# One core: global attention, then a perception layer with local attention; a half of the local values moves between two guide jobs, taps go by a table, bounds are watched by sums of VectorE's own results

## The chip, the cores and the metric

The kernel runs on one core of a Trainium2 chip, in float32. The metric is the device time of one execution in microseconds. A core has TensorE (PE, the matmuls; its weight loads are shown apart as PEld), VectorE (DVE), ScalarE (ACT), GpSimd (POOL) and SyncE (SP, which here only issues DMAs). Each engine works through its own queue in order, and waits on semaphores for the others.

## The reference

Layer 0 is self-attention over the 4096 pixels of each of four images of 64 x 64 x 256. Layer 1 is a depthwise 3x3 convolution with three outputs per channel, an MLP (768 to 512 to 256, gelu) with a residual, and a 3x3 local attention with a residual.

```python
q = x @ Wq + bq; k = x @ Wk + bk; v = x @ Wv + bv
attn = softmax(einsum('bnd,bmd->bnm', q, k), axis=-1)
out = gamma * einsum('bnm,bmc->bnc', attn, v) + inputs          # layer 0

perceived = conv3x3_depthwise(x, w_perc) + b_perc               # 256 -> 768
hid = gelu(einsum('bphw,dp->bdhw', perceived, w_up1) + b_up1)   # 768 -> 512
h = x + einsum('bdhw,cd->bchw', hid, w_up2) + b_up2             # 512 -> 256
q, k, v = split(einsum('bhwc,dc->bhwd', h, w_qkv) + b_qkv, 3)
scores = stack([(q * shifted(k, dy, dx)).sum(-1) for dy, dx in POS]) / 16
out = h + sum(softmax(scores)[i] * shifted(v, *POS[i]))         # layer 1
```

## The kernel before

Pixels lie in 32 blocks of 512 (8 rows of an image), channels on the partitions. The time goes into `unshifted()`, which computes both softmaxes without subtracting a maximum. So that this is safe, it watches its own values: `watch` adds them on GpSimd into a tile `watched`, and at the end a sum of that tile decides whether a second, slower program (`shifted()`, not run here) is needed.

The loop over `slot` handles one block of global attention per slot, in 16 points. At each point TensorE gets, in this order: at even points four `energy` matmuls (`e`, L294), then the jobs of the point, then eight matmul passes of `product` (`acc`, L313). ScalarE takes the exponential of a half of `e` (`p`, L302), VectorE adds `p` into the denominator `den` (L327, one per point). Blocks that are further on run beside it as jobs: with `k = slot - 3`, `hidden_part` (first MLP matmul), `update_part` (second, giving `h`), `guide_part` (query and key weights joined: `lq = wg h`), `scores`, `local_values`, `border`; with `a = slot - 5`, `local_product` and the output. Several of these 2x2 block products are done with seven instead of eight multiplications: `update_part` and `guide_part` have the parts ab, cd, eg, f, and mixes of the inputs are formed on VectorE before (`guide_mix` writes the four `gmix`) and results gathered after (`gather`, L537 and L539).

The convolution (`perceive`) is a generator. Tap 0 of an output runs on ScalarE (L464), each further tap is one scalar_tensor_tensor on VectorE (L468), and four mixes per third (L474) follow: 60 steps per slot. After each point's jobs, product and `den` add, the loop takes steps until `stepped` reaches `to`. So VectorE's queue in a point is: the adds of the point's jobs, the `den` add, the point's taps.

All PSUM banks of jobs come from `job_bank`, and in the loop that is one tag `m` with two buffers, taken in turn: a job's matmul waits until the bank used two jobs ago has been read.

At the end of a slot, `partial_sums` and `finish` turn the denominator into its inverse (`dps`, a matmul of 32 columns), scale `acc` into `o` (L378) and add it to the image in `xp` (L383). `border_terms` and `border` compute the scores that padded neighbours would have: VectorE forms `edge` (L855, L856, four instructions, eight where the block touches the image's upper or lower edge), TensorE sums it over partitions with a matmul by ones (`c`, L867). After the loop, the last blocks go through the same functions with less around them (`run(...)`): there `local_values` of the last block also watches squares of `lv`, and `local_total` sums the local weights on TensorE (`ld`, L994). The three uses of `watch` that the change touches stand in `finish`, `scores` and `local_product`.

Of the kernel before, what the change touches and what calls it, by code (L numbers as in the profile page):

```python
# [15 lines left out]
P = 128  # L16
# [16 lines left out]
MULT = 3  # L33
# [19 lines left out]
def attention_then_perception_kernel(  # L53
# [26 lines left out]
        return t  # L80

    ones = const.tile([P, P], F32, tag="ones", name="ones")
    watched = const.tile([P, C], F32, tag="watched", name="watched")
    bad = const.tile([P, 1], mybir.dt.int32, tag="bad", name="bad")


# [1 line left out]
    def unshifted():  # L88
# [92 lines left out]
        def watch(values):  # L181

            n = values.free_size()
            for i in range(0, n, C):
                at = watched[:, : min(C, n - i)]
                nc.gpsimd.tensor_tensor(at, at, values[:, i : min(n, i + C)], ALU.add)  # L186


        queries, keys, values, staged = {}, {}, {}, {}
# [170 lines left out]
        def finish(s, parts=((0, RB),)):  # L360

            acc = accs.pop(s)
            n = NJ * (1 if shared(s) is None else 2)
            ps = bank("m", f"dps_{s}")[:, :n]
            given = parts_.pop(s).rearrange("p i j -> p (i j)")[:, :n]
            nc.tensor.matmul(ps, lhsT=fold, rhs=given, start=True, stop=True)
            inverse = tile_of([P, 2, NJ], "inverse", f"inverse_{s}")
            inverses[s] = inverse
            nc.vector.reciprocal(inverse.rearrange("p i j -> p (i j)")[:, :n], ps)

            rden = sums.pop(s)[:, 1, :]
            on_all(inverse[:, 0, :], turneds[s][:, 0, :], rden)
            watch(inverse.rearrange("p i j -> p (i j)")[:, :n])
            os = [tile_of([P, NB], "o", f"o_{s}_{c}", 2) for c in range(CH)]
            for r0, r1 in parts:
                n = slice(r0 * W, r1 * W)
                for c, o in enumerate(os):
                    nc.vector.scalar_tensor_tensor(  # L378
                        o[:, n], acc[c][:, n], gam[:, 0:1], rden[:, n], ALU.mult, ALU.mult
                    )  # L380
                for c, o in enumerate(os):
                    dst = xv[:, c, ring(s) + r0 : ring(s) + r1, 1 : 1 + W]
                    nc.vector.scalar_tensor_tensor(  # L383
                        dst, o[:, n].rearrange("p (h w) -> p h w", w=W), gbv[:, c : c + 1], dst,
                        ALU.add, ALU.add,
                    )
                if len(parts) > 1:
                    yield
            if s < NSLOT - 1:
                rim(s)  # L390
            for o in os:
                watch(o)
            yield

        def rim(s):
# [226 lines left out]
        def pixels(s, c):  # L622
            return hs[s][:, c, :, HALO:, :].rearrange("p a h w -> p h a w")
# [39 lines left out]
        def update_part(s, part):  # L663


            if part == "ab":
                below(s)
            b11, b12, b21, b22, mix1 = update_mixes[s]
            y11, y12, y21, y22 = (lambda j, y=y: y[:, j] for y in blocks_of(wup2, CH, P))
            t1, t2, t4 = (lambda j, i=i: wmix2[:, i, j] for i in range(3))  # L670
            v11, v12, v21, v22, v1 = (lambda j, b=b: b[:, j] for b in (b11, b12, b21, b22, mix1))
            todo = dict(
                ab=((y11, v11), (y21, v21)), cd=((t2, v11), (y12, v12)),
                eg=((t1, v1), (t4, v22)), f=((y22, v21),),
            )[part]
            ps = seven(f"dx_{s}_{part}", CH, *todo)
            if part == "ab":
                nc.vector.tensor_tensor(b11, mix1, b11, ALU.subtract)
                nc.vector.tensor_tensor(b21, b21, b11, ALU.subtract)
            gather(  # L680
                part, [by_rows(t) for t in ps],
                *(quarter(s, c, n) for n in range(2) for c in range(2)), None,
            )
            if part == "f":
                for c in range(CH):
                    for half in range(2):
                        h = hs[s][:, c, half, HALO:, :]
                        at = 1 + half * KW
                        nc.vector.scalar_tensor_tensor(
                            h, h, bup2[:, c : c + 1],  # L690
                            xv[:, c, ring(s) : ring(s) + RB, at : at + KW], ALU.add, ALU.add,
                        )
                guide_mix(s)
                border_terms(s)

# [162 lines left out]
        def border(s):  # L860


            ps = job_bank(f"c_{s}")
            row = edge_row(s)
            n_side = 2 * RB
            n = border_parts(s)[-1][0].stop
            nc.tensor.matmul(ps[:, :n], lhsT=ones, rhs=edge[:, :n], start=True, stop=True)  # L867
            one = pad[0:1, :]
            nc.scalar.activation(one[:, :n], ps[0:1, :n], AF.Exp, bias=bc, scale=-(C**-0.5))
            nc.gpsimd.tensor_scalar(one[:, :n], one[:, :n], 3.0, None, ALU.mult)  # L870
            if row is not None:

                ends = one[:, n_side : n : W - 1]
                nc.gpsimd.tensor_scalar(ends, ends, 2.0 / 3.0, None, ALU.mult)
# [39 lines left out]
        def scores(s, half):  # L914
# [19 lines left out]
            else:  # L934
# [7 lines left out]
                    p = late[s][:, half * C : half * C + QR * QW]  # L942
            near_ws[s, half] = p.rearrange("p (t h w) -> p t h w", h=QR, w=QW)
            nc.scalar.activation(p[:, :n], ps[:, :n], AF.Exp, scale=C**-0.5)  # L944
            engine = nc.vector if s >= NSLOT - 2 else nc.gpsimd
            pv = p[:, :n].rearrange("p (t n) -> p t n", t=tiles)
            mask = near[:, half, :rows, :].rearrange("p h w -> p (h w)")
            engine.tensor_tensor(  # L948
                pv, pv, mask.unsqueeze(1).to_broadcast([P, tiles, rows * QW]), ALU.mult
            )  # L950

            if g == 0:
                nc.gpsimd.memset(p[P // 2 :, : UP * QW], 0.0)
                if s < NSLOT:
                    nc.gpsimd.memset(p[: P // 2, UP * QW : QR * QW], 0.0)
            if s >= DIRECT:

                watch(p[:, :n])

# [48 lines left out]
        def local_product(s, c, behind=None):  # L1008
            b, g = divmod(s, NBLK)
            ps = job_bank(f"lo_{s}_{c}")  # L1010
            pv = ps.rearrange("p (h w) -> p h w", w=W)
            todo = [(half, *piece) for half in range(2) for piece in pieces(s)]
            for i, (half, (block, t), rows, of) in enumerate(todo):
                nc.tensor.matmul(  # L1014
                    pv[:, rows, columns(half)],
                    lhsT=lvs[block, t, half][:, bass.ts(c, P)],
                    rhs=near_ws[block, half][:, t, of, :],
                    start=(i == 0), stop=(i == len(todo) - 1), skip_group_check=True,
                )
            if behind:  # L1020
                behind()
            if s < DIRECT:
                o = tile_of([P, NB], "o", f"lo_{s}_{c}", 2)
            else:
                o = tile_of([P, 2, NB], "p", f"lo_{s}_{c}", 3)[:, 0, :]
            nc.vector.tensor_tensor(o, ps, lrdens[s], ALU.mult)  # L1026
            if s < NSLOT - 1:
                watch(o)
            engine, res = nc.gpsimd, o
            if s >= DIRECT:  # L1030

                if c == 0:
                    results[s] = tile_of([P, CH, NB], "xc", f"res_{s}", 2)
                engine, res = nc.vector, results[s][:, c, :]
            ov, rv = (t.rearrange("p (h a w) -> p h a w", a=2, w=KW) for t in (o, res))
            engine.tensor_tensor(rv, ov, pixels(s, c), ALU.add)
            nc.sync.dma_start(out=out[b, :, c, bass.ts(g, NB)], in_=res)

        def job(f, s, *args, n=NSLOT):
            return [lambda: f(s, *args)] if 0 <= s < n else []  # L1040
# [33 lines left out]
        for slot in range(NSLOT):  # L1074
            b, g = divmod(slot, NBLK)
            if slot >= RING:
# [6 lines left out]
                job(hidden_part, k, 1, 0), job(hidden_part, k, 1, 1),  # L1083
                job(local_product, a, 0), job(local_product, a, 1) + job(update_mix, k),
                job(update_part, k, "ab"), job(update_part, k, "cd") + job(update_part, k, "eg"),
                job(update_part, k, "f"), job(guide_part, k, "ab") + job(guide_part, k, "cd"),
                job(guide_part, k, "eg") + job(guide_part, k, "f"), job(scores, k, 0),
                job(scores, k, 1) + job(local_sum, k - 1), job(local_values, k, 0), job(border, k), [],
            ]
            if slot in (1, 2):  # L1090
                jobs[0] = [lambda: next(combine)] * 2
# [7 lines left out]
            conv = perceive(slot - LAG_PERC, mixed) if slot >= LAG_PERC else iter(())  # L1099
            n_mixed = NPC * (TAPS - 1) + MULT * len(MIXED)  # L1100
            n_steps, stepped = n_mixed, 0
            if slot == NSLOT - 1:

                nc.sync.dma_start(out=wup2[:, :CH, P:], in_=w_up2[:, :CH, P:])
# [20 lines left out]
            for point in range(points):  # L1125
# [17 lines left out]
                else:  # L1143
                    partial_sums(slot)

                to = min(n_steps, -(-(point + 1) * n_steps // (points - 2)))
                if point < 3:

                    to = min(to, n_mixed // MULT)
                while stepped < to:  # L1150
                    next(conv, None)
                    stepped += 1
# [492 lines left out]
```

## Time and profile before

| | us |
|---|---|
| Median of three runs | 3489.54 (3489.46 to 3489.93) |
| The profiled execution's own time | 3489.6 |
| Its span, first to last instruction | 3487.6 |
| TensorE busy | 3454.0 |
| VectorE busy | 2796.8 |
| ScalarE busy | 1063.4 |
| GpSimd busy | 694.3 |

The mean granted TensorE clock is 0.999. A slot without projections for the next image lies 103.1 us after the one before by its `dps` matmul, eight of them 104.0; slots 7, 15 and 23, which also project the next image, take 137. In the profile a row of groups gives the line, engine, operation, what is written from what, the number of instructions, the busy time and the mean of one; a float32 matmul shows as two passes, so counts are doubled. In a timeline, the columns are start, length, engine and line, and in brackets the idle time before and what ended it. Matmul ends are modelled and overlap the next start, so the distance from start to start is the better measure of what TensorE takes.

Groups that the change touches:

```profile
L186 POOL TENSOR_TENSOR watched<-watched,lo 128x256 f32<-128x256 f32 x124 | 136.8, 1103 | 1015.8 <-DVE lo L1026 1010.7
L186 POOL TENSOR_TENSOR watched<-watched,o 128x256 f32<-128x256 f32 x128 | 109.6, 856 | 43.2 <-DVE o L378 35.7
L1036 POOL TENSOR_TENSOR lo<-lo,h 128x512 f32<-128x512 f32 x56 | 96.2, 1719 | 4.4
L1026 DVE TENSOR_TENSOR lo<-lo,lrden 128x512 f32<-128x512 f32 x64 | 43.8, 685 | 66.5 <-PE lo L1014 66.2
L378 DVE SCALAR_TENSOR_TENSOR o<-acc,gam,den 128x512 f32<-128x512 f32 x62 | 43.7, 747 | 1.6 <-DVE den L358 0.5
L867 PE MATMUL c<-edge,ones 128*128 128x16 f32 x48 | 9.3, 270 | 0.0
```

### The profile page before, as it was taken

What the parts mean: (1) busy time and instruction counts of PE and PEld (TensorE: products, weight loads), DVE (VectorE), ACT (ScalarE), POOL (GpSimd) and SP (SyncE); (2) the same over time, 40 slices, a digit from 0 to 9 for tenths busy, and PEclk for the clock granted to TensorE, in tenths of its full rate; (3) what the DMA queues carried; (4) which work ended last, traced back from release to release, by engine and by line L of the source; (5) the groups of instructions that cost most, each with busy time, mean ns of one, the idle gap of its engine ahead of it and who ended that gap; (6) DMA issues with size and microseconds to landing.
All of it is one profiled execution on the core that took longest, in us unless ns stands there. A gap on an engine that the chain in (4) does not pass through costs nothing. (4 is left out here: it accounts for less than half of the span.)

```text
span 3487.6 us, 34030 instructions
## 1 busy us (share of the span) xinstructions
PE 3454.0 (99%) x12726; PEld 1995.1 (57%) x12726; DVE 2796.8 (80%) x4249; ACT 1063.4 (30%) x1328; POOL 694.3 (20%) x829
## 2 busy tenths in 40 slices
PE   9999999999999999999999999999999999999998
PEld 5445555555555555566555555556655555555655
DVE  2388888768888988876888889887688888888886
ACT  3233333323332233332333322333233333223331
POOL 2010112111221221121112212212121121221133
PEclk9999999999999999999999999999999999999999
DMA  4000000120000000011000000001100000000000
GB/s 106 7 4 10 7 9 16 32 47 20 9 16 7 16 16 16 22 25 46 16 9 16 10 13 16 16 22 31 39 16 16 16 10 7 16 16 17 7 7 25
DMA packets 93276, 67.06 MB, mean 19 GB/s; under 512 B 65872, under 2 KB 71248, under 8 KB 92976
## 3 DMA queue, kind: packets, MB, share of 16 engines
q1 hardware_dynamic: 92432, 64.42, 6.8%
q8 instruction: 102, 1.67, 0.2%
q14 instruction: 70, 0.57, 0.1%
q10 hardware_dynamic: 672, 0.39, 0.0%
HBM read 43.62 MB, written 18.81 MB: 18 GB/s over the span
## 5 line engine op out<-in xcount | busy, mean ns | idle before, releaser
L313 PE MATMUL acc<-p,v 128*128 128x512 f32 x4096 | 1838.6, 594 | 0.2 <-DVE o L378 0.2
L313 PEld LDWEIGHTS acc<-p,v 128*128 128x128 f32 x4096 | 768.2, 190 | 795.8 <-issue 779.6
L468 DVE SCALAR_TENSOR_TENSOR perc<-xp,wperc,perc 128x512 f32<-128x512 f32 (+2 forms) x1554 | 1166.7, 811 | 7.0 <-ACT perc L464 7.0
L302 ACT ACTIVATE p<-e 128x1024 f32<-128x1024 f32 x512 | 523.9, 1023 | 1695.0 <-PE e L294 776.9
L327 DVE TENSOR_TENSOR den<-den,p 128x1024 f32<-128x1024 f32 x480 | 604.6, 1259 | 85.4 <-ACT p L302 83.6
L186 POOL TENSOR_TENSOR watched<-watched,lo 128x256 f32<-128x256 f32 x124 | 136.8, 1103 | 1015.8 <-DVE lo L1026 1010.7
L948 POOL TENSOR_TENSOR lp<-lp,near 128x396 f32<-128x396 f32 x60 | 77.5, 1291 | 1137.9 <-ACT lp L944 1132.9
L294 PE MATMUL e<-qa,ka 32*128 32x512 f32 x2048 | 291.9, 640 | 0.0
L474 DVE TENSOR_TENSOR perc<-perc 128x256 f32<-128x256 f32 x360 | 174.3, 498 | 7.2
L294 PEld LDWEIGHTS e<-qa,ka 32*128 32x128 f32 x2048 | 80.0, 182 | 166.2 <-issue 164.2
L573 PE MATMUL hid_de<-perc,wmix 128*128 128x256 f32 x720 | 165.2, 379 | 0.0
L573 PEld LDWEIGHTS hid_de<-perc,wmix 128*128 128x128 f32 x720 | 136.8, 190 | 43.7 <-issue 21.5
L580 DVE TENSOR_TENSOR hid<-hid_bc,hid 128x512 f32<-128x512 f32 x60 | 41.5, 692 | 147.4 <-PE hid_bc L573 147.3
L596 ACT ACTIVATE hid<-hid,bup 128x512 f32<-128x512 f32 x120 | 80.1, 715 | 214.3 <-DVE hid L580 214.3
L464 ACT ACTIVATE perc<-xp,bperc,wperc 128x512 f32<-128x512 f32 x192 | 145.4, 807 | 0.0
L969 POOL TENSOR_TENSOR lsum<-lsum,lp 128x99 f32<-128x99 f32 x168 | 132.0, 792 | 11.0
L1014 PEld LDWEIGHTS lo<-lp,lv 128*128 128x128 f32 x732 | 102.9, 191 | 35.1 <-issue 27.0
L883 PE MATMUL lv<-wlv,h 128*128 128x256 f32 x520 | 122.4, 379 | 0.0
L186 POOL TENSOR_TENSOR watched<-watched,o 128x256 f32<-128x256 f32 x128 | 109.6, 856 | 43.2 <-DVE o L378 35.7
L302 ACT ACT_TABLE_LOAD x60 | 77.0, 1283 | 134.1 <-PE e L294 134.1
L260 PE MATMUL v<-wv,xc 128*128 128x256 f32 x512 | 116.3, 380 | 0.1
L883 PEld LDWEIGHTS lv<-wlv,h 128*128 128x128 f32 x520 | 98.7, 190 | 27.5 <-issue 15.5
(191 smaller groups left out, 3398.8 us busy)
## 6 DMA issues: line engine op xcount, KB each, us to landing
xp<-in_x SPq DMA_DIRECT2D x30, 528.0 KB, 4.1
xc<-in_x SPq DMA_DIRECT2D x56, 256.0 KB, 3.7
out<-lo SPq DMA_DIRECT2D x56, 256.0 KB, 2.1
qa<-packed SPq DMA_DIRECT2D x124, 64.0 KB, 2.0
out<-res SPq DMA_DIRECT2D x8, 256.0 KB, 2.0
ka<-st SPq DMA_DIRECT2D x124, 16.0 KB, 1.8
packed<-st SPq DMA_DIRECT2D x31, 64.0 KB, 1.9
wup<-in_w_up SPq DMA_DIRECT2D x1, 1536.0 KB, 6.8
```

The costliest lines, as they stand in the source:

```text
L186: nc.gpsimd.tensor_tensor(at, at, values[:, i : min(n, i + C)], ALU.add)
L260: nc.tensor.matmul(ps[:, i * C : (i + 1) * C], lhsT=xc[:, kin, bass.ts(2 * pair + i, P)], rhs=wv[:, kin, :], start=(kin == 0), stop=(kin = ...
L294: nc.tensor.matmul(e[:, j, :], lhsT=key[rows, :], rhs=queries[s][rows, :], start=True, stop=True,)
L302: nc.scalar.activation(p, energies[s, G][:, 2 * half : 2 * half + 2, :], AF.Exp)
L313: nc.tensor.matmul(accs[s][c], lhsT=v[:, 2 * half + i, bass.ts(c, P)], rhs=p[:, i, :], start=(first and i == 0), stop=(G == NG - 1 and hal ...
L327: nc.vector.tensor_tensor(den, den, p, ALU.add)
L464: nc.scalar.activation(acc, win, AF.Identity, bias=bperc[:, half, j : j + 1], scale=wt)
L468: nc.vector.scalar_tensor_tensor(acc, win, wt, acc, ALU.mult, ALU.add)
L474: nc.vector.tensor_tensor(t[:, to, :], t[:, a, :], t[:, b, :], op)
L573: nc.tensor.matmul(ps[:, n * C : (n + 1) * C], lhsT=w(j), rhs=mixes[s, j][:, kind, :], start=(j == 0), stop=(j == MULT - 1),)
L883: nc.tensor.matmul(ps[:, half * C : (half + 1) * C], lhsT=keys_of(s, t, half, kin), rhs=wlv[:, kin, :], start=(kin == 0), stop=(kin == CH ...
L969: nc.gpsimd.tensor_tensor(to, to, near_ws[block, half][:, t_, of, :], ALU.add)
```

## The change

It has five parts.

- `job(local_values, k, 0)` moves from point 13 to point 9, between the parts ab and cd of `guide_part`. `border_terms` leaves `update_part` (point 8) and becomes the job of point 13.
- In all slots but the last, the steps of the convolution follow a table `share` of steps per point instead of an even division.
- `finish`, `local_product` and, in the last two blocks, `scores` no longer watch on GpSimd. The VectorE instruction that writes the value also writes the sum of what it wrote into a column of `watched` of its own (`accum_out`); tensor_tensor becomes scalar_tensor_tensor for that. What GpSimd still watches, it adds in pieces of 128 columns instead of 256.
- The residual of the local attention runs on VectorE in all blocks, where GpSimd had it in most.
- The matmul `c` of `border` has one column of ones as weights and writes one partition.

```diff
+    WATCHED = P + 4 * NSLOT + 6
+    watched = const.tile([P, WATCHED], F32, tag="watched", name="watched")
...
-            for i in range(0, n, C):
-                at = watched[:, : min(C, n - i)]
-                nc.gpsimd.tensor_tensor(at, at, values[:, i : min(n, i + C)], ALU.add)
+            for i in range(0, n, P):
+                at = watched[:, : min(P, n - i)]
+                nc.gpsimd.tensor_tensor(at, at, values[:, i : min(n, i + P)], ALU.add)
+        free = iter(range(P, WATCHED))
+        def seen():
+            i = next(free)
+            return watched[:, i : i + 1]
...
-                        o[:, n], acc[c][:, n], gam[:, 0:1], rden[:, n], ALU.mult, ALU.mult
+                        o[:, n], acc[c][:, n], gam[:, 0:1], rden[:, n], ALU.mult, ALU.mult,
+                        accum_out=seen(),
...
-            for o in os:
-                watch(o)
...
                 guide_mix(s)
-                border_terms(s)
...
-            nc.tensor.matmul(ps[:, :n], lhsT=ones, rhs=edge[:, :n], start=True, stop=True)
+            nc.tensor.matmul(ps[0:1, :n], lhsT=ones[:, 0:1], rhs=edge[:, :n], start=True, stop=True)
...
-            engine = nc.vector if s >= NSLOT - 2 else nc.gpsimd
+            if s < NSLOT - 2:
+                nc.gpsimd.tensor_tensor(pv, pv, mask, ALU.mult)
+            else:
+                nc.vector.scalar_tensor_tensor(
+                    pv, pv, 1.0, mask, ALU.mult, ALU.mult, accum_out=seen()
+                )
...
-            if s >= DIRECT:
+            if DIRECT <= s < NSLOT - 2:
                 watch(p[:, :n])
...
-            nc.vector.tensor_tensor(o, ps, lrdens[s], ALU.mult)
             if s < NSLOT - 1:
-                watch(o)
-            engine, res = nc.gpsimd, o
+                nc.vector.scalar_tensor_tensor(
+                    o, ps, 1.0, lrdens[s], ALU.mult, ALU.mult, accum_out=seen()
+                )
+            else:
+                nc.vector.tensor_tensor(o, ps, lrdens[s], ALU.mult)
+            res = o
...
-            engine.tensor_tensor(rv, ov, pixels(s, c), ALU.add)
+            nc.vector.tensor_tensor(rv, ov, pixels(s, c), ALU.add)
...
-                job(update_part, k, "f"), job(guide_part, k, "ab") + job(guide_part, k, "cd"),
+                job(update_part, k, "f"),
+                job(guide_part, k, "ab") + job(local_values, k, 0) + job(guide_part, k, "cd"),
                 job(guide_part, k, "eg") + job(guide_part, k, "f"), job(scores, k, 0),
-                job(scores, k, 1) + job(local_sum, k - 1), job(local_values, k, 0), job(border, k), [],
+                job(scores, k, 1) + job(local_sum, k - 1), job(border_terms, k), job(border, k), [],
...
+            share = [6, 7, 7, 5, 4, 3, 3, 3, 2, 2, 4, 5, 5, 4, 0, 0]
...
-                to = min(n_steps, -(-(point + 1) * n_steps // (points - 2)))
-                if point < 3:
-                    to = min(to, n_mixed // MULT)
+                if slot < NSLOT - 1:
+                    to = sum(share[: point + 1])
+                else:
+                    to = min(n_steps, -(-(point + 1) * n_steps // (points - 2)))
+                    if point < 3:
+                        to = min(to, n_mixed // MULT)
```

## The prediction made before the result was known

> **What bounds the kernel now.** I read the page's busy table first, then the waits by engine, then the timelines of TensorE (PE) and VectorE (DVE) through one stretch of 103 us between two `dps` matmuls (one slot), then the timelines of the last 70 us.
>
> ```profile
> PE 3454.0 (99%) x12726; PEld 1995.1 (57%) x12726; DVE 2796.8 (80%) x4249; ACT 1063.4 (30%) x1328; POOL 694.3 (20%) x829
> ```
>
> TensorE is idle for 3487.6 - 3454.0 = 33.6 us of the span. A change that leaves its matmuls alone can win only there. The waits view says where:
>
> ```profile
> PE g_cd L525 <- DVE gmix L798: 13.4, 23, 0.7
> PE s L924 <- DVE lq L539: 5.0, 8, 0.7
> PE ld L994 <- POOL lp L953: 1.8, 1, 1.8
> PE ld L994 <- DVE lp L948: 1.5, 1, 1.5
> PE ld L994 <- DVE lv L948: 1.0, 1, 1.0
> ```
>
> The columns are total, times, longest. The first two recur by slot, the last three stand in the last 75 us. The first is larger than it looks, since a matmul's end is modelled. From the TensorE timeline (slot 20; columns start, length):
>
> ```profile
> 2123.65 1.13 PE L525 MATMUL dx_f<-hid,wup 128*128 128x256 f32 x4
> 2124.61 3.60 PE L313 MATMUL acc<-p,v 128*128 128x512 f32 x8
> 2128.05 1.16 PE L525 MATMUL g_ab<-h,wg 128*128 128x256 f32 x4
> 2129.79 1.10 PE L525 MATMUL g_cd<-gmix,gmix 128*128 128x256 f32 x4 [0.58 <-DVE gmix L798]
> ```
>
> g_ab starts at 2128.05 and g_cd 1.74 later; in the five of 28 slots without the wait it is 0.86. So the stall is 0.88 to 0.90 each, and over all 28 slots these distances exceed 0.86 by 20.7 us in sum. In the same way the eight `acc` before the first `s` take 4.3 instead of 3.43 us in eight slots, 3.51 in most others: 7.4 us in sum. VectorE in the same slot:
>
> ```profile
> 2126.45 0.42 DVE L537 TENSOR_TENSOR h<-dx_f,h 128x256 f32<-128x256 f32 x1
> 2126.79 1.67 DVE L689 SCALAR_TENSOR_TENSOR h<-h,bup,xp 128x256 f32<-128x256 f32 x4
> 2128.55 0.76 DVE L798 TENSOR_TENSOR gmix<-h 128x256 f32<-128x256 f32 x2
> 2129.22 0.42 DVE L798 TENSOR_TENSOR gmix<-gmix,h 128x256 f32<-128x256 f32 x1
> ...
> 2130.83 1.22 DVE L327 TENSOR_TENSOR den<-den,p 128x1024 f32<-128x1024 f32 x1
> ...
> 2133.88 0.48 DVE L539 SCALAR_TENSOR_TENSOR lq<-g_ab,small,lq 128x256 f32<-128x256 f32 x1
> ```
>
> VectorE takes dx_f up at 2126.45 without idling, while TensorE left it at 2124.61: it is 1.64 us behind (in slot 7, 15 and 23, where it idles, it starts 0.20 after). The third gmix ends at 2129.64 and g_cd starts 0.15 later.
>
> **What the Trainium skill says.** "VectorE: DVE Perf Modes", section "Two Vector instructions with no wait between them": an instruction that also writes out its accumulator is two, the main one and an accumulator read. No run here shows it; the nearest tiny VectorE operation, the edge term of 8 elements, takes 0.23 us, 0.15 start to start. "Vector Engine (DVE) Microarchitecture Reference", section "Points that are easy to get wrong", says scalar_tensor_tensor with two non-bf16 SBUF sources halves throughput. The trace doesn't bear this out without a sum: such taps take 0.665 us apart for 512 elements, as tensor_tensor does. "SBUF — State Buffer", section "SBUF: two separate sides", says VectorE with two SBUF inputs and GpSimd lock each other out of a shared port. That agrees: beside GpSimd's watching, four taps at 2106.82 took 3.75 us, 0.94 each.
>
> **Part 1, the table of taps and the work taken to VectorE.** Prices, start to start: tap 0.665, den 1.13, mix step 0.41, 512-wide operation 0.61 (0.72 if it waits for the one before), accumulator read 0.15 to 0.25 (I take 0.2; ends 0 and 0.6, the last if the sum halves the rate). Points 0 to 4 get 29 steps for 22, points 5 to 9 get 13 for 21, points 10 to 13 get 18 for 17. The seven early ones (4.7 us) fall where VectorE idles 0.88 + 0.97 + 0.46 + 4.18 + 1.48 + 1.44 = 9.4 us in this slot. The first hid_de add comes about 0.7 later (2076.6 to 2077.3); its PSUM bank is next wanted at 2081.87. Both versions meet at the hid_gf add at 2094.67, which waits for TensorE. From there, by hand: 2095.3; den 2096.4; ScalarE's first tap of the next tile, behind two gelus, 2097.6; five taps 2100.9; local product 0 with sum and residual (0.61 + 0.2 + 0.72) 2102.5; den 2103.6; four taps 2106.3; product 1 2107.8; two update mixes 2109.2; den 2110.3; three taps 2112.3; dx_ab is ready at 2112.4, three adds 2114.1; den and three taps 2117.2; dx_cd ready 2117.5, then dx_eg ready 2119.25 with three adds 2120.5; den, tap and two mixes 2123.1. dx_f is ready at 2124.8. VectorE therefore waits there 1.7 us where it was 1.64 us late. The residual (56 times 0.7 = 39 us) and the sums (four a slot, 128 x 0.2 = 26 us) are on no path as long as that margin stands. GpSimd loses 136.8 + 109.6 + 96.2 = 343 us, on no path outside the end. The output DMA on SP waits for VectorE at 2102.5 and 2107.8 instead of GpSimd at 2105.7 and 2112.0: earlier, so nothing behind it on that queue is late.
>
> **Part 2, the first half of local values between ab and cd.** It moves four matmuls (eight passes, 1.73 us by L883) and two VectorE adds (0.74) from point 13 into point 9; no DMA. TensorE's count is unchanged. g_cd is now wanted 3.44 + 0.86 + 1.73 = 6.03 us after dx_f's end. gmix is ready by 0.20 + 3.2: far covered. But job banks are two in turn: with the values between, g_cd gets g_ab's bank, so it must wait until VectorE has read g_ab (lq L539). Before it in VectorE's queue: 0.20 latency, dx_f add to last gmix 3.57 (2126.45 to 2130.02), den 1.13, two mixes 0.78, itself 0.48, and 0.15 to TensorE: 6.31. ScalarE's copy of g_ab, which it also needs, ends at 2130.12, that is 5.51: not later. Stall 6.31 - 6.03 = 0.28; I take 0.3 (0 to 0.9). It strikes all 28 slots, the five clean ones too: 8.4, with 0.08 restart in five, 9 us. The wait is shared by everything queued on TensorE. Gain 20.7 - 9 = 11.7 us.
>
> **Part 3, border terms to point 13.** Four or eight operations of 0.23 us leave the way to lq. The lq chain after g_f (three adds, 1.85) ends at 2139.5, and s_0 is due at 2141.3. So the 7.4 us go, the edge slots included. At point 13 the border's matmul follows one point later, over 3 us. The slot's end idles 2.15 us on VectorE; +0.66 for a tap, +0.8 for borders (1.6 in edge slots), -0.74 for the values: hidden.
>
> **Part 4, border sum into one partition.** The two c passes take 0.25 us to the next acc. Weight loads of one column took 81 ns in L753 against 190. I take 0.1 x 32 = 3 us (0 to 4).
>
> **Part 5, the end.** GpSimd is the chain from 3460.65 to 3474.76. The watch of the last block's two `lp` (four rows from 3470.30 to 3473.36, 3.1 us) leaves it; each of six squares is now watched in two pieces of about 0.46 (the row of 140 columns takes 0.56, that of 99 takes 0.40) instead of one of 0.73, + 0.25 with the gap, 1.5 in all; the ld stall of 1.81 falls to about 0.2. The stalls at 3415.6 and 3418.2 give back some 0.4, since GpSimd's watching no longer slows the taps between, less 0.2 for sums. TensorE's clock reads 0.56 and 0.59 in 3419 to 3423: about 1.7 us lost, which I leave standing (gain 0 to 1.7). Together 2 us (0.5 to 4).
>
> **Sum.** 11.7 + 7.4 + 3 + 2 = 24 us from the profiled execution's 3489.6 (span 3487.6 and 2.0 around it), which equals the median shown, 3489.54: 3466.
>
> **Rivals.** (a) The bank wait keeps nearly all of the old stall, because sums cost more or a wait in the queue before lq is longer than read: 28 x 0.7 = 19.6 instead of 9, 3477. For: the chain has thirteen instructions; against: each was measured. (b) No bank wait, lq being early: 9 back, 3457. Against: two banks in turn. (c) Slower: VectorE stays behind at dx_f as now. Every 1 us of delay is 28 us. The gains without the stall are 20.7 + 7.4 + 3 + 2 = 33; at (0.28 + L) x 28 = 33, thus L = 0.9, it is even. At today's L = 1.64 the stall is 1.92, 54 us, which gives 3511. It takes 1.7 + 0.9 = 2.6 us more than I counted between points 3 and 7, where the two sums and two residuals stand; even the sums at half rate bring 0.8. (d) The early taps stall hid banks: they would have to come 4 us later, not 0.7.
>
> **Numbers.** Main case 0.70, 3466 (own range 3460 to 3471); (a) 0.14; (b) 0.08; (c) and (d) 0.05, the rest small gains under 7 us. Range 3456 to 3477. No change means within 0.2%, 7 us, what a measurement can tell here. Faster 0.92, same 0.03, slower 0.05.
>
> **What would show it.** Right: g_cd no longer waits for gmix; a wait of about 0.3 us on lq in all 28 slots, slots of 103.1 and 104.0 us becoming about 102.4 both; VectorE idle before dx_f; no s wait; ld's wait on GpSimd under 0.5. Wrong: VectorE without idle at dx_f, accumulator rows above 0.6 us, or waits of acc or hid on VectorE in points 0 to 3.

## The result and the profile after

The changed kernel takes 3457.85 us (median of four runs, 3457.53 to 3457.90), the kernel before 3489.73 beside it: a ratio of 0.9908, 95% interval 0.9891 to 0.9925. That is 31.9 us less, where the prediction had 24 us and 3466. The profiled execution has a span of 3455.9 us at a granted clock of 0.999, so the spans differ by 31.7 us. The page after, busy times (share of the span) and instruction counts:

```profile
PE 3442.0 (100%) x12726; PEld 1995.0 (58%) x12726; DVE 2736.2 (79%) x4439; ACT 1063.8 (31%) x1328; POOL 355.7 (10%) x525
```

TensorE runs the same 12726 matmul passes and idles 3455.9 - 3442.0 = 13.9 us instead of 33.6; its busy time fell too, by 12 us, so the idle time alone doesn't count the gain. In part that is because a group that runs up to a stall is recorded longer (g_ab in slot 20 had 1.16 us before and has 1.03 now); `c` and `hid` became shorter as well. GpSimd lost half of its work. The waits after (total, times, longest):

```profile
...
PE ld L1005 <- DVE lp L959: 0.8, 1, 0.8
PE g_cd L534 <- DVE lq L548: 0.5, 2, 0.4
...
PE ld L1005 <- POOL lp L964: 0.4, 1, 0.4
```

The two repeated waits of before, of g_cd for gmix and of s for lq, are gone. There is a new releaser of g_cd, the addition to lq at L548. The view counts it twice; the distances from lv to g_cd show it in every slot (1.87 to 2.26 us, where lv alone takes 1.73). TensorE in slot 20 (start, length):

```profile
2107.52 3.60 PE L323 MATMUL acc<-p,v 128*128 128x512 f32 x8
2110.95 1.03 PE L534 MATMUL g_ab<-h,wg 128*128 128x256 f32 x4
2111.82 1.89 PE L891 MATMUL lv<-wlv,h 128*128 128x256 f32 x8
2113.70 1.13 PE L534 MATMUL g_cd<-gmix,gmix 128*128 128x256 f32 x4
2114.67 3.60 PE L323 MATMUL acc<-p,v 128*128 128x512 f32 x8
```

From lv to g_cd it is 1.88 us, where eight passes of lv take 1.73. VectorE in the same slot:

```profile
2107.72 0.42 DVE L546 TENSOR_TENSOR h<-dx_f,h 128x256 f32<-128x256 f32 x1 [1.51 <-PE dx_f L534]
...
2110.89 0.42 DVE L806 TENSOR_TENSOR gmix<-h,gmix 128x256 f32<-128x256 f32 x1
2111.24 1.22 DVE L337 TENSOR_TENSOR den<-den,p 128x1024 f32<-128x1024 f32 x1
2112.37 0.88 DVE L483 TENSOR_TENSOR perc<-perc 128x256 f32<-128x256 f32 x2
2113.17 0.48 DVE L548 SCALAR_TENSOR_TENSOR lq<-g_ab,small,lq 128x256 f32<-128x256 f32 x1
```

VectorE now idles 1.51 us and takes dx_f up 0.20 after TensorE left it (1.84 before). The last gmix is done at 2111.31, over two us before g_cd wants it. The addition to lq ends at 2113.65, and g_cd starts 0.05 later: this is the wait for the bank.

Start-to-start distances on TensorE, summed over the 31 slots between the first and the last `dps`, say where the loop's 28.0 us come from. "Predicted" is the term of the prediction's sum.

| Sites in the loop | before, us | after, us | gain | predicted |
|---|---|---|---|---|
| g_ab, with the wait of g_cd for gmix behind it | 44.8 | 24.2 | 20.6 | 20.7 |
| lv, with the wait of g_cd for the bank | 103.6 | 108.5 | -4.9 | -8.4 |
| g_cd's own extent | 25.9 | 27.1 | -1.2 | -0.4 |
| acc before s, with the wait of s for lq | 107.0 | 99.6 | 7.5 | 7.4 |
| s and g_f, their own extents | 97.4 | 93.0 | 4.4 | 0 |
| c | 7.3 | 4.5 | 2.8 | 3 |
| other acc | 1626.9 | 1627.8 | -0.9 | 0 |

Outside the loop, the stretch from the last `dps` to the end went from 120.2 to 117.0 us, and the start gave 0.5, with a DMA that landed earlier. A slot without projections takes 102.1 us (103.1 before), one at the image's edge 102.2 (104.0), one with projections 137.2 (137.0).

### The profile page after: what moved, and what is told of

The parts are those of the page before. It is cut to its first block, busy times and chain, and to the rows that moved or that the text cites. A ratio compares the mean times of both kernels' runs of the same rounds, so it can differ in the third digit from the quotient of the medians.

```text
span 3455.9 us, 33709 instructions
## 1 busy us (share of the span) xinstructions
PE 3442.0 (100%) x12726; PEld 1995.0 (58%) x12726; DVE 2736.2 (79%) x4439; ACT 1063.8 (31%) x1328; POOL 355.7 (10%) x525
## 4 chain that ended last, share of the span: by engine, by line
PE 98%; DVE 1%; DMA 0%; SPq 0%; ACT 0%; issue 0%; ACTq 0%; POOL 0%; DVEq 0%
PE acc L323 51%; PE e L304 8%; PE hid_de L582 4%; PE hid_gf L582 4%; PE hid_bc L582 4%; PE v L270 3%; PE lv L891 3%; PE lo L1025 3%; PE s L932 3%; PE hid_a L582 3%; PE dx_ab L534 2%; PE dx_cd L534 1%; PE dx_eg L534 1%; PE hid L614 1%; PE g_cd L534 1%; PE qk L236 1%
## 5 line engine op out<-in xcount | busy, mean ns | idle before, releaser
L477 DVE SCALAR_TENSOR_TENSOR perc<-xp,wperc,perc 128x512 f32<-128x512 f32 (+2 forms) x1554 | 1101.2, 770 | 32.4 <-ACT perc L473 32.2
L337 DVE TENSOR_TENSOR den<-den,p 128x1024 f32<-128x1024 f32 x480 | 586.4, 1222 | 86.5 <-ACT p L312 84.7
L957 POOL TENSOR_TENSOR lp<-lp,near 128x396 f32<-128x396 f32 x60 | 96.4, 1607 | 2490.8 <-ACT lp L952 2490.8
L483 DVE TENSOR_TENSOR perc<-perc 128x256 f32<-128x256 f32 x360 | 153.5, 440 | 8.2
L980 POOL TENSOR_TENSOR lsum<-lsum,lp 128x99 f32<-128x99 f32 x168 | 122.3, 735 | 11.0
L270 PEld LDWEIGHTS v<-wv,xc 128*128 128x128 f32 x512 | 97.0, 190 | 28.2 <-issue 15.2
L932 PEld LDWEIGHTS s<-lq,h 128*128 128x128 f32 x520 | 87.1, 188 | 37.3 <-issue 27.4
L1025 PE MATMUL lo<-lp,lv 128*128 128x99 f32 (+1 forms) x732 | 107.4, 295 | 0.0
```

The source lines that it names most:

```text
L270: nc.tensor.matmul(ps[:, i * C : (i + 1) * C], lhsT=xc[:, kin, bass.ts(2 * pair + i, P)], rhs=wv[:, kin, :], start=(kin == 0), stop=(kin = ...
L337: nc.vector.tensor_tensor(den, den, p, ALU.add)
L477: nc.vector.scalar_tensor_tensor(acc, win, wt, acc, ALU.mult, ALU.add)
L483: nc.vector.tensor_tensor(t[:, to, :], t[:, a, :], t[:, b, :], op)
L932: nc.tensor.matmul(ps[:, t * QR * QW : t * QR * QW + rows * QW].rearrange("p (h w) -> p h w", w=QW), lhsT=keys_of(s, t, half, kin), rhs=gu ...
L1025: nc.tensor.matmul(pv[:, rows, columns(half)], lhsT=lvs[block, t, half][:, bass.ts(c, P)], rhs=near_ws[block, half][:, t, of, :], start=(i ...
```

## The experiments

Every kernel was measured beside the kernel before on the same chip (medians there 3489.45 to 3490.95). Times are medians. One caution for differences below 2 us: the 96 passes of `hid` after the loop take 42.2 to 42.3 us in some profiles and 43.8 to 45.0 in others, of kernels with the same code there, because the granted clock drops for some microseconds in the second case (to 0.79 over 3381 to 3389 us in e1's profile, where the same passes have 1.00 after the change). So versions within 2 us of each other are compared by their loops.

**The place of the local values, and the table.** Four versions take the change apart. `e1_values_at_13` puts the moved half back to point 13:

```diff
-                job(guide_part, k, "ab") + job(local_values, k, 0) + job(guide_part, k, "cd"),
+                job(guide_part, k, "ab") + job(guide_part, k, "cd"),
-                job(scores, k, 1) + job(local_sum, k - 1), job(border_terms, k), job(border, k), [],
+                job(scores, k, 1) + job(local_sum, k - 1), job(local_values, k, 0) + job(border_terms, k), job(border, k), [],
```

> The changed kernel with one part undone: the first half of the local values stands at point 13 again (before the border terms), so the parts ab and cd of guide_part are neighbours. Theory T (the table of taps brings VectorE in time to dx_f, and the moved values only cost): gmix is ready 0.20 + 3.2 + 0.15 us after dx_f, wanted after 4.30, so no stall of g_cd; the 0.15 us in front of g_cd and the 0.11 of its slower start go in 28 slots, 7 us: about 3451. If the 0.74 us of value adds at point 13 make dps late, some of it is lost, 3451 to 3455. Rival R1 (the moved values are what covers the wait for gmix): the stall of 0.9 us a slot returns, 28 x 0.63 net: about 3475.

Measured: 3450.49 us (3449.74 to 3451.92), ratio 0.9885 (0.9868 to 0.9901). That is 7.4 us faster than the whole change. In the loop lv is back at 103.6 and g_cd at 24.2 us, all other sites are as after the change. The move costs; it removes nothing that isn't gone without it.

`e4_values_at_10` puts the moved half ahead of guide part eg instead:

```diff
-                job(guide_part, k, "eg") + job(guide_part, k, "f"), job(scores, k, 0),
+                job(local_values, k, 0) + job(guide_part, k, "eg") + job(guide_part, k, "f"), job(scores, k, 0),
```

> The changed kernel with the first half of the local values at the start of point 10, before eg, instead of between ab and cd. There VectorE waits 2.2 us for eg, and the bank of the values has been read by then. Theory T: no stall in front of g_cd, none in front of f (VectorE reads the values 0.95 us after them, f is wanted after 0.97): 28 x 0.26 = 7 us less than the changed kernel, about 3451, and not more than the run with the values at 13. Rival: f or s waits for the values' bank, 0.2 us or more a slot: 3456 or more.

Measured: 3458.67 us (3457.69 to 3459.59), ratio 0.9908. A miss for the first reading: the loss only moved. Now g_f waits until VectorE has read lv from the bank. The weight load of g_f in slot 20 of e4:

```profile
2120.74 0.30 PEld L534 LDWEIGHTS g_f<-gmix,wg 128*128 128x128 f32 x2 [0.39 <-DVE lv L904]
```

In each slot lv's extent grows by 0.10 us, g_f's by 0.10 and g_eg's by 0.04, together 0.24, where the place between ab and cd costs 0.28. (The wait lies in g_eg's distance; its other 0.10, which the first group behind `e` takes longer, has gone over to lv.) Three groups in a row through two banks wait at both places.

`e2_even_taps` keeps the whole change but gives the taps out evenly, as before:

```diff
-                if slot < NSLOT - 1:
-                    to = sum(share[: point + 1])
-                else:
-                    to = min(n_steps, -(-(point + 1) * n_steps // (points - 2)))
-                    if point < 3:
-                        to = min(to, n_mixed // MULT)
+                to = min(n_steps, -(-(point + 1) * n_steps // (points - 2)))
+                if point < 3:
+                    to = min(to, n_mixed // MULT)
```

> The changed kernel with the even division of taps in all slots instead of the table. Theory T: VectorE is about 1.6 us late at dx_f again and two residuals later still (up to 3 us, less what GpSimd no longer slows), g_cd waits for lq, 1.5 to 2.5 us in 23 slots: 3488 to 3512, no faster than the kernel before. Rival R1 (the moved values cover it): within 3 us of the changed kernel, 3458 to 3461. Rival R2 (GpSimd's watching was what made VectorE late): also 3458 to 3462.

Measured: 3492.78 us (3491.9 to 3495.66, 12 runs), ratio 1.0006 (0.9997 to 1.0015): the whole gain is lost. Its waits:

```profile
PE g_cd L534 <- DVE lq L548: 34.9, 28, 1.6
```

The time met the expectation, and I took it at first for proof that without the table VectorE is late at dx_f as before. The releaser says otherwise: it isn't gmix that g_cd waits for but the bank. VectorE starts on dx_f 1.31 us after its first product, against 1.17 with the table and 2.82 before. It is 0.14 us late, not 1.64, which e10 below shows to be too little to stall g_cd. But between gmix and the addition to lq stand four steps of the convolution now, not two, so this addition starts 6.90 us after TensorE has left dx_f and not 5.65, and lv's extents sum to 143.1 us.

`e3_table_alone` is the kernel before with only the table:

```diff
+            share = [6, 7, 7, 5, 4, 3, 3, 3, 2, 2, 4, 5, 5, 4, 0, 0]
...
-                to = min(n_steps, -(-(point + 1) * n_steps // (points - 2)))
-                if point < 3:
-                    to = min(to, n_mixed // MULT)
+                if slot < NSLOT - 1:
+                    to = sum(share[: point + 1])
+                else:
+                    to = min(n_steps, -(-(point + 1) * n_steps // (points - 2)))
+                    if point < 3:
+                        to = min(to, n_mixed // MULT)
```

> The kernel before with the table of taps alone; nothing else of the change. Theory T: g_cd loses its stall (20.7 us by start to start distances), most of the 7.4 us before s goes too since four taps fewer stand before lq at points 8 and 9, and s starts cleanly; the c matmuls (3 us) and the end (3 us) stay as before: 3459 to 3464. Rival R1: VectorE in time is not enough, the stall of g_cd stays at 0.5 us or more a slot: 3475 or more. Rival R2: VectorE is still late at dx_f beside GpSimd's watching: 3480 or more.

Measured: 3455.64 us (3455.35 to 3455.81), ratio 0.9900 (0.9884 to 0.9917). That is 3.4 us below the expected range, and the table alone beats the whole change by 2 us (in the loop by 6.2: 3222.0 against 3228.3). Both stalls are gone; also s and g_f are 4.4 us shorter in sum, which the expectation didn't count. VectorE idles before dx_f although GpSimd still does all of its work. Slot 20 of e3:

```profile
2103.91 0.42 DVE L537 TENSOR_TENSOR h<-dx_f,h 128x256 f32<-128x256 f32 x1 [0.80 <-PE dx_f L525]
```

**The smaller parts, and what the table must do.** `e5_c_all_columns` is the version at point 13 with border's product by all of `ones`:

```diff
-            nc.tensor.matmul(ps[0:1, :n], lhsT=ones[:, 0:1], rhs=edge[:, :n], start=True, stop=True)
+            nc.tensor.matmul(ps[:, :n], lhsT=ones, rhs=edge[:, :n], start=True, stop=True)
```

> The changed kernel with the local values at point 13 (the version that took 3450.5 us), and in it border's product with all 128 columns of ones again in place of one. T, the column is worth what the two traces show of c in the regular slots (0.24 us from its start to the next group before, 0.13 after, 28 such slots and a few smaller ones): 28 x 0.11 = 3.1 us slower, 3453.0 to 3454.0. Rival, the difference is only where the trace puts the boundary between c and the groups of acc around it (the 16 of acc before dps took 6.94 us in the kernel with the table alone, 6.97 after the change): 0 to 1.2 us, 3450 to 3451.7.

Measured: 3452.20 us (3451.42 to 3454.0), loop 3222.1 us against 3220.4. Between both readings: one column is worth 1.8 us, not 2.8. A third of what c's distances show goes into the `acc` around it.

`e6_sums_on_gpsimd` is the same version with o, lo and the residual as before the change:

```diff
-                        accum_out=seen(),
...
+            for o in os:
+                watch(o)
...
+            nc.vector.tensor_tensor(o, ps, lrdens[s], ALU.mult)
             if s < NSLOT - 1:
-                nc.vector.scalar_tensor_tensor(
-                    o, ps, 1.0, lrdens[s], ALU.mult, ALU.mult, accum_out=seen()
-                )
-            else:
-                nc.vector.tensor_tensor(o, ps, lrdens[s], ALU.mult)
-            res = o
+                watch(o)
+            engine, res = nc.gpsimd, o
...
-            nc.vector.tensor_tensor(rv, ov, pixels(s, c), ALU.add)
+            engine.tensor_tensor(rv, ov, pixels(s, c), ALU.add)
```

> The same version (3450.5 us) with the loop's watching of o and lo and the local residual back on GpSimd, while the sums of the last two slots' masks stay on VectorE. T, these sums and residuals were never on the path that sets the end of a slot, on either engine: 3449.0 to 3452.0, and the slots keep 101.8 us. Rival 1, the sums cost VectorE time that TensorE waits for: faster, below 3449. Rival 2, GpSimd's watching slows VectorE's taps (0.93 us for the xp step before, 0.74 after) until h is late at dx_f again: 3453 or more, with a wait of g_cd for gmix back in the list of waits.

Measured: 3450.90 us (3450.01 to 3451.89), loop 3220.3. As expected: in this version, with the table, it makes no difference to the time which engine does this work.

`e7_room_for_lq` is the changed kernel with its two steps of point 8 given at point 9:

```diff
-            share = [6, 7, 7, 5, 4, 3, 3, 3, 2, 2, 4, 5, 5, 4, 0, 0]
+            share = [6, 7, 7, 5, 4, 3, 3, 3, 0, 4, 4, 5, 5, 4, 0, 0]
```

> The changed kernel as it is, local values between ab and cd, with the table's two steps at point 8 (those that VectorE runs just before the first addition to lq, 0.88 us in all) put to point 9. T, g_cd waits for the bank that this addition frees: it is over 0.8 us earlier, ahead of the end of lv, so that lv's extent goes from 3.61 back to 3.45 us and g_cd's from 0.97 to 0.87: 28 x 0.26 = 7.3 us faster than the changed kernel, 3450 to 3452, the local values' place costs nothing any more. Rival, the added group costs for itself (the third bank's turn, the load of other weights, the additions of blv that follow it): 3456.5 to 3458.5. The deciding point is 3454.

Measured: 3454.89 us (one run at 3458.35, the others 3454.49 to 3455.05): 3 us of 7.4. That lies in neither range, 0.9 us on the rival's side of the deciding point: the addition's place in the queue was only a part of the wait. The groups view of e7 says what is late next (busy, mean ns; then idle before):

```profile
L548 DVE SCALAR_TENSOR_TENSOR lq<-g_ab,small,lq 128x256 f32<-128x256 f32 x28 | 13.4, 479 | 16.8 <-ACT lq L552 16.8
```

VectorE is free for the addition and idles 16.8 us in 28 slots, 0.6 each, for ScalarE's copy of g_ab's first half, which the addition needs. In the changed kernel this idle time is 0.1 us in all. ScalarE in slot 20 of e7:

```profile
2109.72 1.02 ACT L312 ACTIVATE p<-e 128x1024 f32<-128x1024 f32 x1 [3.44 <-PE acc L323]
2110.64 0.50 ACT L774 COPY lq<-lq 128x384 f32<-128x384 f32 x1
2111.17 0.37 ACT L552 COPY lq<-g_ab 128x256 f32<-128x256 f32 x1
```

g_ab is complete at 2110.33, but the copy L552 stands behind the copy of lq's upper rows, L774, that `guide_above` issues in the same job. `e9_guide_above_earlier` adds to e7 that this copy is given out one point earlier:

```diff
             if part == "ab":
-                guide_above(s)
...
-                job(update_part, k, "f"),
+                job(update_part, k, "f") + job(guide_above, k),
```

> The changed kernel with the table's two steps at point 8 moved to point 9 (3454.9 us: there the first addition to lq waited 0.6 us a slot for ScalarE's copy of g_ab, which stands behind ScalarE's copy of lq's upper rows, 0.50 us), and now that copy of the upper rows given out one point earlier, after dx_f. T, g_cd's bank is freed by a chain of two engines, ScalarE's copy of a and VectorE's addition of b; with both queues cleared it comes 0.5 us before the end of lv, g_cd waits no more (lv 3.45 us, g_cd 0.87) and the local values' place between ab and cd costs nothing: 3450 to 3451.8. Rival, the place itself costs (g_cd stays 0.1 us longer than after ab, whatever it waits for): 3453.0 to 3455.5.

Measured: 3451.89 us (3450.03 to 3452.11), 0.1 above the expected range by the median; loop 3220.5 us, lv 103.6 and g_cd 24.2 in sum, as at point 13. With both queues cleared the place costs nothing. So the 7.4 us were the bank's wait, along a chain of two engines: g_ab, copy on ScalarE, addition on VectorE. And even so it brings nothing.

`e8_light_before_guides` is the version at point 13 with a flatter table:

```diff
-            share = [6, 7, 7, 5, 4, 3, 3, 3, 2, 2, 4, 5, 5, 4, 0, 0]
+            share = [5, 5, 5, 5, 5, 5, 4, 3, 2, 3, 4, 5, 5, 4, 0, 0]
```

> The version with the local values at point 13 (3450.5 us) with a table that is even up to point 5 (5 steps each), then 4, 3, 2, 3 and 4, 5, 5, 4: by the end of point 8 it has given out 39 steps, as the even rule had, where the table of the change had 40, but only 9 of them at points 6 to 8 (13 by the even rule, 8 by the change's table). T, what counts is how little is queued on VectorE at points 6 to 8, just ahead of the addition of dx_f and of gmix: 3450 to 3453. Rival, VectorE falls behind earlier, at points 3 to 5 (with 15 steps there against 12), and what it hasn't done by then makes it late at dx_f: g_cd waits for gmix again, 3456 to 3485, the size telling how much of the backlog is carried.

Measured: 3450.01 us (3449.68 to 3450.1), ratio 0.9885 (0.9869 to 0.9902). The expectation held, but the run tells less than I meant it to: the next kernel has no table at all and is as fast, so in this version the test had little to fail at: the even rule itself makes nothing late.

**Is the table needed at all?** `e10_rest_without_table` is the version at point 13 with the edit of e2, the even rule.

> The version with the local values at point 13 (3450.5 us) with the even rule in place of the table: all of the change but its table and its moved values. T1, the table alone makes the gain, so that g_cd's wait for gmix and s's for lq are back: 3478 to 3486. T2, there are two sufficient causes. In the kernel before, the addition of dx_f starts 2.82 us after dx_f's first product, with the table 1.17, and with the change's even version 1.31; this comes from GpSimd's watching and residual of lo, beside which VectorE's steps ran at 1.21 us for 0.70 and 0.91 for 0.44. Without these gmix is ready 3.9 us after dx_f, before g_ab ends at 4.3, and nothing waits once the local values aren't between ab and cd: 3450 to 3454. The deciding point is 3465.

Measured: 3450.67 us (3449.92 to 3451.83), ratio 0.9888 (0.9871 to 0.9904). T2 held. Every site of the loop is as with the table (3220.4 us in all). TensorE in slot 20 of e10:

```profile
2102.72 3.60 PE L323 MATMUL acc<-p,v 128*128 128x512 f32 x8
2106.15 1.03 PE L534 MATMUL g_ab<-h,wg 128*128 128x256 f32 x4
2107.02 1.03 PE L534 MATMUL g_cd<-gmix,gmix 128*128 128x256 f32 x4
```

g_cd follows g_ab after 0.87 us, without a wait. VectorE in the same slot:

```profile
2103.06 0.42 DVE L546 TENSOR_TENSOR h<-dx_f,h 128x256 f32<-128x256 f32 x1
```

It takes dx_f up without idling, 0.34 us after TensorE left it, so it is 0.14 late, and the last gmix is still done at 2106.65. What made VectorE late before is seen some 20 us earlier in its slot. Before, GpSimd at the first local product:

```profile
2101.82 2.44 POOL L186 TENSOR_TENSOR watched<-watched,lo 128x256 f32<-128x256 f32 x2 [32.04 <-DVE lo L1026]
2104.33 1.33 POOL L1036 TENSOR_TENSOR lo<-lo,h 128x512 f32<-128x512 f32 x1
```

and VectorE beside it, in the same kernel:

```profile
2102.72 1.81 DVE L474 TENSOR_TENSOR perc<-perc 128x256 f32<-128x256 f32 x2
2104.46 2.42 DVE L468 SCALAR_TENSOR_TENSOR perc<-xp,wperc,perc 128x512 f32<-128x512 f32 x2
```

The same four steps in e10, behind the product with its sum and the residual that VectorE now adds itself:

```profile
2079.02 0.69 DVE L1038 SCALAR_TENSOR_TENSOR lo<-lo,lrden 128x512 f32<-128x512 f32 x1 [1.51 <-PE lo L1025]
2079.64 0.08 DVE L1038 DVE_READ_ACCUMULATOR lo<-lo,lrden 128x1 f32 x1
2079.75 0.69 DVE L1050 TENSOR_TENSOR lo<-lo,h 128x512 f32<-128x512 f32 x1
...
2081.49 0.88 DVE L483 TENSOR_TENSOR perc<-perc 128x256 f32<-128x256 f32 x2
2082.29 1.41 DVE L477 SCALAR_TENSOR_TENSOR perc<-xp,wperc,perc 128x512 f32<-128x512 f32 x2
```

The pairs take 1.81 and 2.42 us beside GpSimd's work and 0.88 and 1.41 without. Over both local products of that slot the longer steps (1.81 for 0.88, 2.42 for 1.41, 1.10 for 0.69, 1.74 for 1.22, 3.74 for 2.73) cost VectorE 3.9 us; the residual costs it 1.4. "SBUF — State Buffer", section "SBUF: two separate sides" of the Trainium skill, says that the port pair shared by VectorE and GpSimd is an exclusive lock. The trace agrees that they hinder each other, on both sides: the four watching instructions took 788 to 1570 ns each, where the shortest of their kind in this profile takes 722. Whether one fully blocks the other or both only run slower, these durations don't tell. Waiting for GpSimd's results is not the cause: the waits view of the kernel before has no wait of VectorE for GpSimd.

`e11_lo_on_vector_alone` tests this on the kernel before, with this one part of the change (and GpSimd's remaining watching in strips of 128 columns, not 256):

```diff
-            nc.vector.tensor_tensor(o, ps, lrdens[s], ALU.mult)
             if s < NSLOT - 1:
-                watch(o)
-            engine, res = nc.gpsimd, o
+                nc.vector.scalar_tensor_tensor(
+                    o, ps, 1.0, lrdens[s], ALU.mult, ALU.mult, accum_out=seen()
+                )
+            else:
+                nc.vector.tensor_tensor(o, ps, lrdens[s], ALU.mult)
+            res = o
...
-            engine.tensor_tensor(rv, ov, pixels(s, c), ALU.add)
+            nc.vector.tensor_tensor(rv, ov, pixels(s, c), ALU.add)
```

> The kernel before with one edit: the local results are watched by the sums of VectorE's own products, and their residual is added on VectorE; no table, local values at point 13, o and the masks watched by GpSimd, border's terms and product as before. T2, this alone takes GpSimd's work from beside the steps ahead of dx_f, the addition of dx_f comes about 1.3 us after dx_f, the waits for gmix and lq vanish: 3453 to 3461 (the gain of 32 to 35 us, less what the edge slots keep). T1, only the table helps: 3483 to 3490. Rival 3, half, since o's watching at the slot's start delays VectorE too: 3462 to 3478.

Measured: 3464.16 us (3462.79 to 3465.14), ratio 0.9926 (0.9909 to 0.9942), inside rival 3's range by the time alone, and outside T2's. Its waits:

```profile
PE ld L1003 <- POOL lp L962: 4.6, 1, 4.6
PE s L934 <- DVE lq L549: 1.6, 7, 0.5
```

The loop took 3225.9 us instead of 3256.2, a gain of 30.3: the wait for gmix gave its 20.6 in full, and only the edge slots keep 0.5 us each, a wait of s for lq behind the eight border terms. So T2 holds for the loop. Rival 3 doesn't: o is still watched by GpSimd, and before the first local product VectorE waits 1.4 us for `hid_gf` here as it did before, so nothing that o's watching delays earlier in the slot, in wide strips or narrow ones, reaches dx_f. What T2 hadn't in it is the end, 126.4 us against 120.2. Of these 6.2 us, 3.8 lie in `ld`, 1.1 in `hid` (at the lower clock) and 0.7 in `lo`. The wait of ld for GpSimd grew from 1.8 to 4.6 us: squares and masks are still watched there, in 46 rows of 24.4 us for the narrower strips, where it had been 24 rows of 18.0.

The four corners side by side, medians in us:

| | values at point 13 | values between ab and cd |
|---|---|---|
| even rule, the rest as before | 3489.5 | not run |
| table, the rest as before (e3) | 3455.6 | not run |
| even rule, the rest of the change (e10, e2) | 3450.7 | 3492.8 |
| table, the rest of the change (e1, after) | 3450.5 | 3457.9 |

Several versions beat both kernels. The simplest, e10, leaves out the table and the move; e8 has the lowest median, 3450.01. They can't be told apart.

## Why the prediction was right, and where it was off

The result lies in the range, and the sites were the right ones. What the prediction wanted to see is there: no wait for gmix, slots of 103.1 and 104.0 us now nearly equal (102.1 and 102.2, where 102.4 was predicted), VectorE idle before dx_f (1.7 predicted, 1.51 measured), no wait of s in the loop, ld's wait for GpSimd 0.4 (under 0.5). The two old stalls came out at 20.6 and 7.5 us (20.7 and 7.4 predicted).

The terms that were mis-sized explain the missing 8 us:

- **Part 2, the stall for the bank.** It was predicted at 0.28 us, taken as 0.3, and measured at 108.5 - 103.6 = 4.9 over 28, or 0.18 (0.15 in nearly all slots, 0.5 and 0.3 in two). Of the chain, the step from VectorE to TensorE was the wrong one: 0.05 us (2113.65 to 2113.70), not 0.15. The start of the chain was right: the addition to lq begins 5.65 us after TensorE has left dx_f, 5.68 by the prediction's sum. The restart, by which g_cd itself is longer after a wait, was counted in the five clean slots alone, 0.08 each; it is 0.10 in all 28, but 23 of them had paid one for gmix already. Together 6.1 us lost, not 9.
- **Part 3, the wait of s.** Only the stall ahead of s was counted. s itself starts cleanly now, 2.79 instead of 2.95 us in a regular slot, and so does g_f in the edge slots (0.43 instead of 0.53): 4.4 us more.
- **Part 5, the end.** 3.2 us instead of 2. The clock's drop, left standing at "gain 0 to 1.7", wasn't in this profile: `hid` took 42.3 us, not 43.9. That 1.6 is luck as far as the runs show, since e1 with the same code there has 43.9; without it the end gives 1.6, less than predicted. The ld waits gave 1.81 - 0.39 for GpSimd and 1.51 - 0.77 for VectorE.
- **Part 4.** 3 us was predicted; c's distances give 2.8, but e5 shows 1.8, and the 0.9 us by which other `acc` grew is about the rest.

The step that failed is in the account of causes, and no total shows it. Part 2 books "Gain 20.7 - 9 = 11.7 us" for the moved values, with gmix "far covered" by them. In e1 gmix needs no cover: with VectorE on time it is ready before g_ab ends. The move had nothing to gain, and cost 7.4 us. Part 1 treats the sums and the residual as added load that "are on no path as long as that margin stands", a margin made by the table. That they are on no path is right (e6). But taking this work from GpSimd gives VectorE the time by itself (e10, and in the loop e11). The prediction had seen taps of 0.94 us beside GpSimd, and its sum by hand from 2094.67 on takes every tap at 0.665 and every mix step at 0.41: the relief is in that sum, but unnamed, and goes to the table's account. (Those taps stand at 2110.80 in the trace, 3.74 us, not at 2106.82, and in part beside the second residual on GpSimd, not its watching.) Slot 20 tells the two apart: VectorE is 1.64 us late at dx_f before, 0.14 late with the relief alone (e10), 0.80 early with the table alone (e3), 1.51 early with both. By the prediction's own figures some 0.75 us of lateness costs nothing, an estimate: g_ab ends 4.30 us after TensorE leaves dx_f, and gmix needs 0.20 + 3.2 + 0.15 of them. So table and relief are two sufficient cures for the wait for gmix; neither is needed beside the other. The table is needed only where the move is made: there the even rule costs 34.9 us (e2 against after), through the bank's wait alone.

Rival (b), 3457 with no bank wait, is nearest in time and wrong in mechanism: the wait is there. Rival (c) had the right lever, delay times 28, but in e2 the delay stands behind gmix, not ahead of dx_f.

## What to carry to other kernels

When a change bundles several cures for one stall, take each away alone and also leave each alone: removing one from the full set (e2) read as proof for the table, until the releaser of the wait named another cause. Filling a stall with other work was worth nothing here once its cause was gone, and a third group through two banks added a wait of its own, as long as either engine that must read the bank first came late. And work on an idle engine isn't free if its rows lengthen those of the engine that is late.

## What the runs showed of the hardware

A sum taken along by a product costs VectorE almost nothing here. The accumulator read shows with 0.08 us, and the product with sum takes 687 ns where it took 685 without; the next instruction starts 0.73 us after the product (2079.02 to 2079.75), the read included. The prediction took 0.2 for the read. It also left open whether a sum halves the rate with two SBUF sources. The masks of the last two blocks are such a case, and don't show it: 571 ns (median of three products of `lv` by `near`, 396 elements) with the sum, 570 without it before.

A group that had to wait is itself longer. Its first weight load isn't ahead of it any more. Weight loads of TensorE in e1, where g_cd's product starts at 2107.53:

```profile
2107.32 0.84 PEld L534 LDWEIGHTS g_cd<-gmix,gmix 128*128 128x128 f32 x4
```

and after the change, where its product starts at 2113.70:

```profile
2113.70 0.73 PEld L534 LDWEIGHTS g_cd<-gmix,gmix 128*128 128x128 f32 x4 [0.40 <-DVE lq L548]
```

The load starts 0.21 us before its product in the first, together with it in the second, and the group's extent is 0.86 and 0.97 us. "TensorE: Matmul & The Clock Gate", section "Step-by-step: what each phase is for", says that loads are pulled ahead of running matmuls, so that the next tile's weights load while this tile's matmul runs; the load whose data or bank is late loses this. Over 28 slots it is 0.1 us each for g_cd. The 4.4 us of s and g_f above fit it: in slot 20 the first load of s stood with its product at 2140.23 before, and stands 0.43 ahead of it after (2123.67 and 2124.10), and that group of s takes 1.34 us instead of 1.50.
